# Transposing x1 by DMA in the first three batch entries of a fused linear-attention and FP4-FFN kernel

## The chip, the cores and the metric

The kernel runs on one core of one Trainium2 chip. Its time is the device time of one execution in microseconds (us). Three runs of the kernel before took 1883.41, 1884.52 and 1885.26 us, so the median is 1884.52 us. The core has five engines with a queue each: TensorE (PE in the profile, with its weight loads as PEld), VectorE (DVE), ScalarE (ACT), GpSimd (POOL) and SyncE (SP), which here issues nearly all DMAs. Everything is computed in float32 except the quantized grids.

## The reference

The input `src` has 4 batch entries of 2048 rows and 256 columns. Cut to what matters:

```
xn = (src - mean) / sqrt(var + eps)               # per row
# attention branch
Q, K = elu(xn @ Wq + bq) + 1, elu(xn @ Wk + bk) + 1   # 16 heads of 64
KV = einsum('bshd,bshm->bhdm', K, xn @ Wv + bv)
o  = Q KV / (Q . sum(K) + eps)
x1 = layer_norm(xn + o @ Wo + bo) * g1 + be1
y  = gelu(x1 @ W1 + b1) @ W2 + b2
s  = layer_norm(x1 + y) * g2 + be2
# gate branch: weights and activations quantized to FP4 in blocks of 16
h  = silu(q(xn) @ q(w_gate).T) * (q(xn) @ q(w_up).T)
out = src + s * silu(q(h) @ q(w_down).T)
```

The change bears on `x1`: how its affine part is applied, how it is transposed for `x1 @ W1`, and what is issued around it.

## The kernel before

Rows are worked in 32 blocks of 256 (two tiles of 128 rows, `j` = 0 and 1); a batch entry has 8 blocks. A prologue works the keys of entry 0. Then a loop over `n` = 0 to 31 does the queries, attention and both FFNs of block `n`, and, while there is a next entry, two "subs" of that entry's keys beside it. Each entry has 16 subs: the first eight make the normalized rows `xn_k` and their transpose `xnT_k` (keys of the first 512 features), the last eight load both back from DRAM (second 512 features). So in the blocks before a block with `bi` = 0 to 3 keys are normalized and transposed too; in the other blocks of entries 0 to 2 they are only loaded. Blocks 24 to 31 (the last entry) have no keys beside them.

The order on PE is the order of the program's text (`tc.keep_in_program_order`). In the steady loop VectorE, ScalarE, GpSimd and SP are put in order by a scheduler at build time, with `tc.issue_after` as the author's hints; in the prologue VectorE and ScalarE too keep the program's order. The result is a fixed order per queue: an instruction that waits holds up all that stand behind it on its engine.

Per block PE does, in order and by the names of its PSUM tiles: `pk` (keys), `pz` (row sums for the denominators), `pxk` (keys times rows), `pg` (gate and up), `pd` (down), a second `pk`, `pa` (attention times Wo; by seven products over sums `zs` of VectorE in entries 0 to 2), `pxk`, part of `py` (x1's second FFN product of block `n-1`), `pt_x` (the transposes of x1), `pscale` (the transpose of the FP4 scales), the rest of `py`, `pq` (queries of block `n+1`), `pf` (x1 @ W1). PSUM has eight banks; four of them go round among all `mm` tiles, so `pq` and `pf` also wait until VectorE or ScalarE has read out the tile that had the bank before.

After `pa`, VectorE adds the parts into `x1` (`add_seven`), takes mean and variance (`stats`, with a power on GpSimd for 1/sqrt, tile `rstd`), and normalizes. `x1_T` then transposes the normalized x1 by four PE transposes into `pt_x`, and ScalarE copies it out with scale g1 and bias be1. GpSimd applies the same affine part to the row-major x1 (`ffn_addend`: times g1, plus `shift`, which is be1 + b2). GpSimd also makes `o = g*be2 + x` and `g*g2` for the output (`gate_addend`), and adds bo to xn (`attention_addend`). VectorE uses `o` and `g` in `output_of`.

`keys_apart` and `keys_T` are the way in which 22 of the key tiles are transposed: ScalarE copies the high and low 16-bit halves of the float32 tile apart, a DMA transposes them, and ScalarE puts the halves together again.

Of the kernel before, what the change touches and what calls it, by code (L numbers as in the profile page):

```python
# [8 lines left out]
F32 = mybir.dt.float32  # L9
# [6 lines left out]
P = 128  # L16
LN_EPS = 1e-5
Z_EPS = 1e-6
BLK = 16
# [3 lines left out]
def linear_attention_gated_by_fp4_ffn(  # L23
# [158 lines left out]
    for _ in range(24):  # L182
# [13 lines left out]
    W2_OF = {"11": 0, "21": 1, "22": 2, "t1": 3, "t2": 4, "t3": 5, "t4": 6}  # L196
    row_tiles = {
        name: const.tile([P, 1, D], F32, name=f"{name}_r")
        for name in ("bo", "g1", "shift", "g2", "be2")
    }  # L200
    rows = {name: t.to_broadcast([P, TB, D]) for name, t in row_tiles.items()}

# [3 lines left out]
    def load_row(name, v, dep):  # L206
        load_when(dep, row_tiles[name][:, 0, :], as_rows(v))
# [10 lines left out]
    def w2_sums():  # L218
# [23 lines left out]
            lambda dep: load_row("shift", be1, dep),  # L242
            lambda dep: load_row("g2", g2, dep),
            lambda dep: load_row("be2", be2, dep),
        ],
# [18 lines left out]

    cols = {}

    def add_b2(dep):
        b2_r = work.tile([P, D], F32, tag="s", name="b2_r", bufs=1)
        load_when(dep, b2_r, as_rows(b2))
        shift = row_tiles["shift"][:, 0, :]  # L270
        nc.gpsimd.tensor_tensor(shift, shift, b2_r, ALU.add)

    def small_constants():


        vs = (("b1", b1), ("g1", g1), ("be1", be1))
        n = sum(v.shape[0] // P for _, v in vs)
        brow = work.tile([n, P], F32, tag="z", name="brow", bufs=1)
        r = 0
        for name, v in vs:  # L280
            k = v.shape[0] // P
            nc.sync.dma_start(brow[r : r + k, :], v.rearrange("(c p) -> c p", p=P))
            cols[name] = (r, r + k)
            r += k
        yield
        pb = mm_tile("pb")
        tr(pb[:, :n], brow, ident[:n, :n])
        bcol = const.tile([P, n], F32, name="bcol")
        vector.tensor_copy(bcol, pb[:, :n])
        for name, (lo, hi) in cols.items():  # L290
            cols[name] = bcol[:, lo:hi]
        yield


# [2 lines left out]
    def fp4_scale(x, am, name):  # L297

        nb = x.shape[1]
        rs = small.tile([P, I // BLK], F32, tag="rs", name=f"rs_{name}")[:, :nb]  # L300
        vector.tensor_reduce(am, x, AX.X, ALU.max, apply_absolute_value=True)
        vector.tensor_scalar(am, am, -1.0 / 6.0, -1e-12, ALU.mult, ALU.min)
        vector.reciprocal(rs, am)
        return rs
# [146 lines left out]

    xn_d, xnT_d = {}, {}
    keys = {}

# [42 lines left out]
            nc.sync.dma_start(xn, xn_d[n])  # L499
            nc.sync.dma_start(xnT, xnT_d[n])  # L500

    def keys_apart(b, sub, issue=None):
# [7 lines left out]
        half = keys[b, sub][0].bitcast(U16).rearrange("p j (c f h) -> p h c j f", c=ND, h=2)  # L510
        apart = work.tile([P, 2, ND, TB, P], U16, tag="e", name=f"apart_{n}", bufs=3)
        with tc.issue_after(issue) if issue is not None else nullcontext():
            for h in range(2):
                scalar.copy(apart[:, h], half[:, h])
        apartT = work.tile([P, 2, ND * T], U16, tag="kk", name=f"apartT_{n}", bufs=3)
        nc.sync.dma_start(
            apartT.rearrange("p h (m t) -> p (h m) t", t=P),
            apart.rearrange("p h c j f -> p (h c j f)"),
            transpose=True,
        )  # L520
        keys[b, sub].append(apartT)

    def keys_T(b, sub, issue=None):

        f, bi = divmod(sub, NB)
        if f > 0:
            return
        n = b * NB + bi
        xn, *apartT = keys[b, sub]
        xnT = work.tile([P, ND, T], F32, tag="xnT_k", name=f"xnT_k_0_{n}", bufs=3)  # L530
        if apartT:
            with tc.issue_after(issue):
                scalar.copy(
                    xnT.bitcast(U16).rearrange("p c (t h) -> p h (c t)", h=2), apartT[0]
                )
# [241 lines left out]
    def down(n, j):  # L777
        if j == 0:
            blk[n]["pd"] = acc_tile(f"pd_{n}").rearrange("p (j d) -> p j d", j=TB)
        pd = blk[n]["pd"]  # L780
        for i in range(NI):
            mm(
                pd[:, j, :], qT[:, i, j * P : (j + 1) * P], wd[:, i, :], start=i == 0, stop=i == NI - 1
            )
        if j < TB - 1:
            return
        g = work.tile([P, TB, D], F32, tag="g", name=f"g_{n}")
        scalar.activation(g, pd, AF.Silu)
# [22 lines left out]
    def ffn_addend(n, behind=True):  # L811

        x1 = blk[n]["x1"]
        with tc.issue_after(pool["last"]) if behind else nullcontext():
            nc.gpsimd.tensor_tensor(x1, x1, rows["g1"], ALU.mult)
            pool["last"] = nc.gpsimd.tensor_tensor(x1, x1, rows["shift"], ALU.add).ins


    def q_of(n, chunks=range(NH)):
# [128 lines left out]
            vector.tensor_tensor(x1, xn, pa, ALU.add)  # L948
        blk[n]["x1"] = x1

    def attention_norm(n):
        x1 = blk[n]["x1"]
        mv, rstd = stats(x1, f"1_{n}")
        normalize(x1, x1, mv, rstd)

    def x1_T(n):
        x1 = blk[n]["x1"]
        pt = transposes(x1, f"x1_{n}")
        x1T = work.tile([P, ND, T], F32, tag="x1T", name=f"x1T_{n}", bufs=1)
        for c in range(ND):  # L960
            ins = scalar.activation(
                x1T[:, c, :], pt[:, c, :], AF.Identity,
                bias=cols["be1"][:, c : c + 1], scale=cols["g1"][:, c : c + 1],
            )
        blk[n]["x1T"] = x1T
        blk[n]["act"] = ins.ins

    def ffn_1(n, chunks=range(NF)):
        x1T = blk[n]["x1T"]
# [80 lines left out]
    for n in range(NB):  # L1050
# [47 lines left out]
        ready = weight  # L1098
        if n == 4:
            w_down_sb = load_down()  # L1100
        if n == 5:
            add_b2(dep)
        if n == 6:
            load_xn(0)
            scales_x(0)
# [49 lines left out]
    for n in range(NBLK):  # L1155
        b, bi = divmod(n, NB)
        subs = (2 * bi, 2 * bi + 1) if b + 1 < B else ()
        if n < last:
            gate = gate_up(n + 1)
        if 1 < n < last:  # L1160
            gate_addend(n - 1)
        if subs:
            if n == 0:
# [25 lines left out]
            down(n, 1)  # L1189
        elif n < last:  # L1190
            load_xnT(n + 1)
            block_addends(n)
            with tc.issue_after(quantized_h(n, 0).ins):
                ins = quantized_x(n)
            ins = sums(n, ins.ins)
            down(n, 0)
            with tc.issue_after(ins.ins):
                quantized_h(n, 1)
            step(m_half)
            step(gate, 9)  # L1200
            step(m_half)
            down(n, 1)
        else:
            for j in range(TB):
                quantized_h(n, j)
                down(n, j)
        with tc.issue_after(blk[n + 1]["late"]) if n < last else nullcontext():
            qz_ins = qz(n)
        if in_seven(b):
            attention_sums(n)  # L1210
        if not subs:
            ffn_2(n - 1, 4 if n < last else 8)
        if n == 0:
            attention(n)
        kk_ins = keys_k(b + 1, subs[1]) if subs else qz_ins
        if n > 0:
            with tc.issue_after(kk_ins):
                ffn_sums(n - 1)
            attention(n)
        with tc.issue_after(kk_ins):  # L1220
            attention_norm(n)
        if n + 2 < NBLK:
            load_xn(n + 2)
        if subs:
# [31 lines left out]
        if n > 0:  # L1256
            ffn_2(n - 1, 28)
        if more[0]:
            q_of(n + 1)
        if more[0]:  # L1260
            grid_of_h(n + 1, 0)
            grid_T(n + 1, 0, NI)
# [9 lines left out]
            step(m_half)  # L1272
        for sub in next_subs[:1]:
            keys_T(bn + 1, sub, blk[n + 1]["exp"])
        if n + 1 == last:
            ffn_1(n, range(2))
            sums(last)
            ffn_1(n, range(2, NF))
            gpsimd_behind(blk[n]["hT"][:, NF - 1, :])
            gate_addend(n)  # L1280

            w2_last = wk_sb.rearrange("p c (e d) -> p (c e) d", d=D)
            nc.sync.dma_start(w2_last, by_chunks(W2))
        else:
            ffn_1(n)
# [46 lines left out]
```

## Time and profile before

| | |
|---|---|
| median of three runs | 1884.52 us |
| the profiled execution's own time | 1883.6 us |
| its span | 1881.8 us |
| PE busy | 1860.8 us (99%) |
| VectorE busy | 1381.8 us (73%) |
| ScalarE busy | 706.5 us (38%) |
| GpSimd busy | 382.5 us (20%) |
| granted TensorE clock | 0.999 |

The page's chain of work that ended last lies on PE for 77% of the span. A block of entries 0 to 2 takes about 56.4 us, a block of the last entry 44.4 us (the distance of equal PE rows in the chain). Idle time of an engine that is not on that chain costs nothing by itself. The end of a matmul is modelled in this profile, so a busy PE row can hide a short wait; the starts are measured, and the distance of two starts tells what a matmul took of PE.

### The profile page before, as it was taken

What the parts mean: (1) busy time and instruction counts of PE and PEld (TensorE: products, weight loads), DVE (VectorE), ACT (ScalarE), POOL (GpSimd) and SP (SyncE); (2) the same over time, 40 slices, a digit from 0 to 9 for tenths busy, and PEclk for the clock granted to TensorE, in tenths of its full rate; (3) what the DMA queues carried; (4) which work ended last, traced back from release to release, by engine and by line L of the source; (5) the groups of instructions that cost most, each with busy time, mean ns of one, the idle gap of its engine ahead of it and who ended that gap; (6) DMA issues with size and microseconds to landing.
All of it is one profiled execution on the core that took longest, in us unless ns stands there. A gap on an engine that the chain in (4) does not pass through costs nothing.

```text
span 1881.8 us, 25202 instructions
## 1 busy us (share of the span) xinstructions
PE 1860.8 (99%) x9324; PEld 1382.2 (73%) x9324; DVE 1381.8 (73%) x2524; ACT 706.5 (38%) x1190; POOL 382.5 (20%) x363
## 2 busy tenths in 40 slices
PE   8999999999999999999999999999999999999998
PEld 4456677777777777777777787777777788888887
DVE  5676677766677877777677787776776777888875
ACT  2343544324334335443233543353323333333332
POOL 1411322011122212220112221222101122222212
PEclk9999999999999999999999999999999999999999
DMA  5525655444535456635344654564443444444542
GB/s 182 194 77 127 116 120 102 100 102 94 96 63 99 111 98 122 143 66 110 81 89 79 119 100 104 94 139 90 91 88 71 104 77 83 89 83 84 92 83 50
DMA packets 229433, 188.77 MB, mean 100 GB/s; under 512 B 107687, under 2 KB 191155, under 8 KB 229310
## 3 DMA queue, kind: packets, MB, share of 16 engines
q1 hardware_dynamic: 228476, 185.58, 47.4%
q8 instruction: 74, 1.21, 0.3%
q10 hardware_dynamic: 834, 1.58, 0.3%
q14 instruction: 49, 0.40, 0.1%
HBM read 131.96 MB, written 32.59 MB: 87 GB/s over the span
## 4 chain that ended last, share of the span: by engine, by line
PE 77%; DVE 10%; DMA 9%; SPq 1%; issue 1%; POOL 1%; ACT 1%; POOLq 0%; DVEq 0%; ACTq 0%
PE pg L103 14%; PE pk L103 10%; PE pxk L103 10%; PE pf L103 9%; PE pa L103 8%; PE pq L103 8%; PE pd L103 7%; PE py L103 7%; DMA zb<-z_d 2%; DMA qT<-scale_d 2%; PE pz L103 1%; DMA xn_d<-xn_k 1%; DMA z_d<-z 1%; DVE x L119 1%; POOL rstd L430 1%
## 5 line engine op out<-in xcount | busy, mean ns | idle before, releaser
L430 POOL TENSOR_TENSOR rstd<-rstd,neg_half 128x2 f32<-128x2 f32 (+1 forms) x97 | 77.3, 797 | 1324.8 <-DVE rstd L119 964.9
L103 PE MATMUL pg<-wgu,qT 128*128 128x352 f32 x1024 | 308.5, 459 | 0.2 <-PE pm L103 0.2
L103 PEld LDWEIGHTS pg<-wgu,qT 128*128 128x128 f32 x1024 | 194.3, 190 | 113.8 <-issue 11.5
L103 PE MATMUL pk<-wk_sb,xnT_k 128*128 128x512 f32 x512 | 230.4, 592 | 1.2 <-ACT xnT_k L119 1.2
L103 PE MATMUL pf<-x1T,w_sb 128*128 128x256 f32 x1024 | 227.7, 380 | 2.2 <-DVE zq L119 1.6
L103 PE MATMUL pxk<-kk,xn_k 128*128 128x512 f32 x496 | 227.9, 598 | 1.1 <-DVE kk L119 1.1
L103 PE MATMUL pq<-xnT,wq_sb 128*128 128x256 f32 x1024 | 227.6, 380 | 0.9 <-DVE zq L119 0.8
L103 PEld LDWEIGHTS pf<-x1T,w_sb 128*128 128x128 f32 x1024 | 193.6, 190 | 32.3 <-DVE zq L119 6.0
L103 PEld LDWEIGHTS pq<-xnT,wq_sb 128*128 128x128 f32 x1024 | 191.8, 190 | 27.1 <-DVE zq L119 2.4
L119 DVE SCALAR_TENSOR_TENSOR kk<-ek,pk 128x512 f32<-128x512 f32 x128 | 85.5, 684 | 170.3 <-ACT ek L119 170.3
L103 PE MATMUL pd<-wd,qT 128*128 128x256 f32 x768 | 172.9, 380 | 1.1 <-DVE qT L119 1.1
L119 ACT ACT_TABLE_LOAD x121 | 155.2, 1283 | 49.2 <-PE pk L103 34.3
L103 PEld LDWEIGHTS pk<-wk_sb,xnT_k 128*128 128x128 f32 x512 | 97.0, 190 | 102.6 <-issue 90.3
L119 ACT ACTIVATE x1T<-pt_x,bcol 128x256 f32<-128x256 f32 x64 | 32.6, 560 | 357.8 <-PE pt_x L106 357.8
L103 PEld LDWEIGHTS pd<-wd,qT 128*128 128x128 f32 x768 | 145.3, 190 | 27.9 <-DVE qT L119 4.4
L103 PEld LDWEIGHTS pxk<-kk,xn_k 128*128 128x128 f32 x496 | 89.4, 190 | 99.2 <-issue 87.0
L119 DVE TENSOR_TENSOR h<-h,pg 128x352 f32<-128x352 f32 x128 | 66.0, 516 | 105.4 <-PE pg L103 103.2
L119 ACT ACTIVATE h<-pg 128x352 f32<-128x352 f32 x128 | 58.8, 459 | 211.3 <-PE pg L103 211.2
L119 ACT ACTIVATE hT<-pf,bcol 128x256 f32<-128x256 f32 x256 | 105.7, 471 | 66.0 <-PE pf L103 65.6
L119 DVE TENSOR_TENSOR zq<-zq,zb 128x1024 f32<-128x1024 f32 x64 | 79.2, 1238 | 64.9 <-DMA zb<-z_d 64.5
L103 PE MATMUL py<-w_sb,hs 128*128 128x128 f32 x992 | 122.0, 275 | 0.0
L119 ACT ACTIVATE e<-pq,neg_one 128x512 f32<-128x512 f32 x128 | 86.6, 685 | 84.7 <-PE pq L103 70.6
(159 smaller groups left out, 2789.4 us busy)
## 6 DMA issues: line engine op xcount, KB each, us to landing
zb<-z_d SPq DMA_DIRECT2D x128, 256.0 KB, 6.3
qT<-scale_d SPq DMA_DIRECT2D x248, 128.0 KB, 6.0
x_k<-in_L_attn_src_dram SPq DMA_DIRECT2D x32, 256.0 KB, 4.0
x<-in_L_attn_src_dram SPq DMA_DIRECT2D x32, 256.0 KB, 2.9
xn_d<-xn_k SPq DMA_DIRECT2D x32, 256.0 KB, 2.7
xn<-xn_d SPq DMA_DIRECT2D x32, 256.0 KB, 2.7
xnT_d<-xnT_k SPq DMA_DIRECT2D x32, 256.0 KB, 2.0
xnT<-xnT_d SPq DMA_DIRECT2D x32, 256.0 KB, 4.0
```

The source lines that it names most:

```text
L103: return tc.keep_in_program_order(nc.tensor.matmul(*args, **kw))
L119: ins = op(*args, **kw)
L430: pool["last"] = nc.gpsimd.tensor_tensor(rstd[:, j0:j1], rstd[:, j0:j1], neg_half[:, j0:j1], ALU.pow).ins
```

## The change

1. `x1_T` of blocks 1 to 23 no longer uses PE. ScalarE copies the 16-bit halves of x1 apart (`apart`), one DMA transposes them, and ScalarE puts them together (`x1_together`), in the middle of the query products of the next block. The buffers are parts of the tile `zs`.
2. g1 and be1 are applied by VectorE in `attention_norm`: two `scalar_tensor_tensor` per tile in the place of one `tensor_scalar`. GpSimd only adds b2. Blocks 0 and 24 to 31 still transpose x1 on PE, with one plain copy on ScalarE.
3. Of two keys in one block, the second is copied apart and transposed later, behind the queries; the first takes the third part of the `zs` tile.
4. In the last entry, GpSimd's `gate_addend` waits for the quantized h (`qT`), where it stood behind the previous block's output.
5. In block 0 the FP4 scales of the second tile stand behind the sums `zs`, the key normalization behind x1's, and a one-element Exp on ScalarE follows the Silu of `down`.
6. The last block's attention is done tile by tile (`attention_by_tiles`).

```diff
@@ fp4_scale
-        rs = small.tile([P, I // BLK], F32, tag="rs", name=f"rs_{name}")[:, :nb]
+        rs = small.tile([P, I // BLK], F32, tag="rs", name=f"rs_{name}", bufs=3)[:, :nb]
...
+    def apart(x, xp, xpT):
+        half = x.bitcast(U16).rearrange("p j (c f h) -> p h c j f", c=ND, h=2)
+        for h in range(2):
+            ins = scalar.copy(xp[:, h], half[:, h])
+        nc.sync.dma_start(
+            xpT.rearrange("p h (m t) -> p (h m) t", t=P),
+            xp.rearrange("p h c j f -> p (h c j f)"),
+            transpose=True,
+        )
+        return ins.ins
+
+    def together(xT, xpT, issue):
+        with tc.issue_after(issue):
+            scalar.copy(xT.bitcast(U16).rearrange("p c (t h) -> p h (c t)", h=2), xpT)
...
@@ down
-        scalar.activation(g, pd, AF.Silu)
+        blk[n]["silu"] = scalar.activation(g, pd, AF.Silu).ins
...
@@ ffn_addend
-            nc.gpsimd.tensor_tensor(x1, x1, rows["g1"], ALU.mult)
-            pool["last"] = nc.gpsimd.tensor_tensor(x1, x1, rows["shift"], ALU.add).ins
+            pool["last"] = nc.gpsimd.tensor_tensor(x1, x1, rows["b2"], ALU.add).ins
...
+    def attention_by_tiles(n):
+        x1 = blk[n]["x1"] = work.tile([P, TB, D], F32, tag="x1", name=f"x1_{n}")
+        xn, zq = blk[n].pop("xn"), blk[n].pop("zq")
+        for j in range(TB):
+            pa = (acc_tile, mm_tile)[j](f"pa{j}_{n}")[:, :D]
+            for c in range(NH):
+                mm(
+                    pa, zq[:, c, j * P : (j + 1) * P], m_sb[n // NB, c // FOUR][:, c % FOUR, :],
+                    start=c == 0, stop=c == NH - 1,
+                )
+            vector.tensor_tensor(x1[:, j, :], xn[:, j, :], pa, ALU.add)
+            attention_norm(n, (j,))
+
-    def attention_norm(n):
+    def attention_norm(n, js=range(TB)):
         x1 = blk[n]["x1"]
-        mv, rstd = stats(x1, f"1_{n}")
-        normalize(x1, x1, mv, rstd)
+        mv, rstd = stats(x1, f"1_{n}_{js[0]}", js)
+        for j in js:
+            vector.scalar_tensor_tensor(
+                x1[:, j, :], x1[:, j, :], mv[:, j, 0:1], rows["g1"][:, j, :], ALU.subtract, ALU.mult
+            )
+        for j in js:
+            ins = vector.scalar_tensor_tensor(
+                x1[:, j, :], x1[:, j, :], rstd[:, j : j + 1], rows["be1"][:, j, :], ALU.mult, ALU.add
+            )
+        blk[n]["normal"] = ins.ins
+
+    def x1_by_dma(n):
+        return n > 0 and in_seven(n // NB)
 
     def x1_T(n):
         x1 = blk[n]["x1"]
-        pt = transposes(x1, f"x1_{n}")
-        x1T = work.tile([P, ND, T], F32, tag="x1T", name=f"x1T_{n}", bufs=1)
-        for c in range(ND):
-            ins = scalar.activation(
-                x1T[:, c, :], pt[:, c, :], AF.Identity,
-                bias=cols["be1"][:, c : c + 1], scale=cols["g1"][:, c : c + 1],
-            )
-        blk[n]["x1T"] = x1T
-        blk[n]["act"] = ins.ins
+        x1T = blk[n]["x1T"] = work.tile([P, ND, T], F32, tag="x1T", name=f"x1T_{n}", bufs=1)
+        if x1_by_dma(n):
+            t = work.tile([P, 3, ND * T], F32, tag="zs", name=f"apart_x1_{n}", bufs=1).bitcast(U16)
+            xp, blk[n]["room"] = (
+                t[:, i].rearrange("p (h c j f) -> p h c j f", h=2, c=ND, j=TB) for i in (0, 2)
+            )
+            blk[n]["apart"] = t[:, 1].rearrange("p (h t) -> p h t", h=2)
+            blk[n]["act"] = apart(x1, xp, blk[n]["apart"])
+        else:
+            blk[n]["act"] = scalar.copy(x1T, transposes(x1, f"x1_{n}")).ins
+
+    def x1_together(n, issue):
+        if x1_by_dma(n):
+            together(blk[n]["x1T"], blk[n].pop("apart"), issue)
...
@@ loop over n
-        if 1 < n < last:
+        if 1 < n < last and subs:
             gate_addend(n - 1)
...
         elif n < last:
             load_xnT(n + 1)
+            ins = quantized_h(n, 0)
+            gpsimd_behind(qT[:, 0, :])
+            gate_addend(n - 1)
             block_addends(n)
-            with tc.issue_after(quantized_h(n, 0).ins):
+            with tc.issue_after(ins.ins):
                 ins = quantized_x(n)
...
         if n == 0:
             attention(n)
+            one = small.tile([1, 1], F32, tag="one", name="one_exp")
+            with tc.issue_after(blk[n]["silu"]):
+                scalar.activation(one, neg_one[:1], AF.Exp)
...
-            attention(n)
-        with tc.issue_after(kk_ins):
-            attention_norm(n)
+            if n < last:
+                attention(n)
+            else:
+                attention_by_tiles(n)
+        if n < last:
+            with tc.issue_after(kk_ins):
+                attention_norm(n)
...
-            with tc.issue_after(qz_ins) if not subs else nullcontext():
+            behind = zs_ins if n == 0 else None if subs else qz_ins
+            with tc.issue_after(behind) if behind is not None else nullcontext():
                 scales_h(n + 1, 1)
...
+        x1_T(n)
         for sub in next_subs if n == 0 else ():
-            keys_in(bn + 1, sub)
-        x1_T(n)
+            with tc.issue_after(blk[n]["normal"]):
+                keys_in(bn + 1, sub)
...
-        for sub in next_subs:
-            keys_apart(bn + 1, sub, blk[n]["act"])
+        room = blk[n].pop("room", None)
+        for sub in next_subs[:1]:
+            keys_apart(bn + 1, sub, blk[n]["act"], room)
...
-            q_of(n + 1)
+            q_of(n + 1, range(NH // 2))
+            x1_together(n, blk[n + 1]["exp"])
+            q_of(n + 1, range(NH // 2, NH))
...
+        for sub in next_subs[1:]:
+            keys_apart(bn + 1, sub, blk[n + 1]["exp"])
```

Left out are the row tiles (`be1` and `b2` loaded as two rows in the place of their sum `shift`), the smaller table of column constants, and `keys_apart` and `keys_T`, which now call `apart` and `together`.

More of the change, by code (lines that the diff above doesn't have):

```diff
@@ L198, in linear_attention_gated_by_fp4_ffn @@
         name: const.tile([P, 1, D], F32, name=f"{name}_r")
-        for name in ("bo", "g1", "shift", "g2", "be2")
+        for name in ("bo", "g1", "be1", "b2", "g2", "be2")
     }
@@ L241, in linear_attention_gated_by_fp4_ffn @@
             lambda dep: load_row("g1", g1, dep),
-            lambda dep: load_row("shift", be1, dep),
+            lambda dep: load_row("be1", be1, dep),
+            lambda dep: load_row("b2", b2, dep),
             lambda dep: load_row("g2", g2, dep),
@@ L265, in linear_attention_gated_by_fp4_ffn @@
     cols = {}
[L267 to L271, printed above, removed]
-    def small_constants():
[L276 to L284, printed above, removed]
+    def small_constants():
+        brow = work.tile([NF, P], F32, tag="z", name="brow", bufs=1)
+        nc.sync.dma_start(brow, b1.rearrange("(c p) -> c p", p=P))
         yield
         pb = mm_tile("pb")
[L287 to L291, printed above, removed]
+        tr(pb[:, :NF], brow, ident[:NF, :NF])
+        cols["b1"] = const.tile([P, NF], F32, name="bcol")
+        vector.tensor_copy(cols["b1"], pb[:, :NF])
         yield
@@ L500, in keys_in, with keys_apart @@
             nc.sync.dma_start(xnT, xnT_d[n])
-    def keys_apart(b, sub, issue=None):
+    def keys_apart(b, sub, issue=None, xp=None):
         f, bi = divmod(sub, NB)
@@ L509, in keys_apart @@
         n = b * NB + bi
-        half = keys[b, sub][0].bitcast(U16).rearrange("p j (c f h) -> p h c j f", c=ND, h=2)
-        apart = work.tile([P, 2, ND, TB, P], U16, tag="e", name=f"apart_{n}", bufs=3)
+        if xp is None:
+            xp = work.tile([P, 2, ND, TB, P], U16, tag="e", name=f"apart_{n}", bufs=3)
+        apartT = work.tile([P, 2, ND * T], U16, tag="kk", name=f"apartT_{n}", bufs=3)
         with tc.issue_after(issue) if issue is not None else nullcontext():
[L513 to L519, printed above, removed]
-        )
+            apart(keys[b, sub][0], xp, apartT)
         keys[b, sub].append(apartT)
@@ L531, in keys_T @@
         if apartT:
[L532 to L535, printed above, removed]
+            together(xnT, apartT[0], issue)
         else:
@@ L1100, in linear_attention_gated_by_fp4_ffn @@
             w_down_sb = load_down()
-        if n == 5:
-            add_b2(dep)
         if n == 6:
@@ L1209, in linear_attention_gated_by_fp4_ffn @@
         if in_seven(b):
-            attention_sums(n)
+            zs_ins = attention_sums(n)
         if not subs:
@@ L1248, in linear_attention_gated_by_fp4_ffn @@
             gate_addend(n)
-        for sub in next_subs:
-            keys_apart(bn + 1, sub, blk[n]["act"])
+        room = blk[n].pop("room", None)
+        for sub in next_subs[:1]:
+            keys_apart(bn + 1, sub, blk[n]["act"], room)
+        room = None
         if n > 0 and not subs:
```

## The prediction

> **What bounds the kernel now.** I read the page's busy times first, then PE's waits, then the timeline of one block.
>
> ```profile
> span 1881.8 us, 25202 instructions
> ...
> PE 1860.8 (99%) x9324; PEld 1382.2 (73%) x9324; DVE 1381.8 (73%) x2524; ACT 706.5 (38%) x1190; POOL 382.5 (20%) x363
> ```
>
> PE is busy 99%, VectorE 73%. The waits of PE alone (columns: us in total, times, longest):
>
> ```profile
> PE pa L103 <- DVE zs L119: 2.4, 3, 1.6
> ...
> PE pf L103 <- DVE zq L119: 1.6, 3, 0.8
> ...
> PE pt_x L106 <- DVE x L119: 1.1, 3, 0.5
> ```
>
> All of PE's visible waits come to some 14 us, so what is taken out of PE's queue shortens the run unless a wait takes its place. The timeline of block 3 (start, length):
>
> ```profile
> 360.70 0.73 DVE L119 TENSOR_SCALAR x<-x,mv,rstd 128x256 f32<-128x256 f32 x2 [0.81 <-POOL rstd L430]
> 361.32 1.95 PE L103 MATMUL py<-w_sb,hs 128*128 128x128 f32 x16
> ...
> 363.11 0.60 PE L106 MATMUL pt_x<-ident,x 128*128 128x128 f32 x4
> 363.55 0.27 PE L106 MATMUL pscale<-ident,scale 128*128 128x128 f32 x1
> ...
> 365.44 7.07 PE L103 MATMUL pq<-xnT,wq_sb 128*128 128x256 f32 x32
> ...
> 372.35 1.89 PE L103 MATMUL pf<-x1T,w_sb 128*128 128x256 f32 x8
> ```
>
> From 361.3 to 379 PE has no gap. The four transposes take 363.55 - 363.11 = 0.44 us, 0.109 us each by their starts. x1 was ready at 361.43 and is wanted, transposed, at 372.35: there is room for a slower way.
>
> [...] But the starts carry no slack: 32 `pq` matmuls follow each other every 6.91/32 = 0.216 us. [...]
>
> **1. Transposes out of PE, blocks 1 to 23.** 23 x 0.436 = 10.0 us. PE also waited for x1 in five of these blocks (starts at 479, 536, 881, 939 and 1342 us): 0.26 + 0.37 + 0.60 + 0.58 + 0.84 = 2.65 us. Nothing on PE needs x1 there any more, so I count 12.7 us.
>
> What has to hide instead, with the block above and PE 0.44 earlier after the transposes:
> - VectorE: four operations like `s<-s,mv,g` for two like `x<-x,mv,rstd`, some 1.1 us a block on an engine that is busy 73%; uncovered, 25 us over these blocks.
>
> ```profile
> L119 DVE SCALAR_TENSOR_TENSOR s<-s,mv,g 128x256 f32<-128x256 f32 x62 | 30.2, 492 | 0.0
> ...
> L119 DVE TENSOR_SCALAR x<-x,mv,rstd 128x256 f32<-128x256 f32 x64 | 23.5, 410 | 20.4 <-POOL rstd L430 20.4
> ```
>
> In the changed order one g1 operation stands ahead of the power's input (+0.42), the other beside the power (+0.15, see 3), two be1 operations behind it (+0.17), and `y` moves behind x1 (-0.61). x1 is ready near 361.6.
> - ScalarE copies the halves apart: 1.14 us a pair in this trace. To 362.8.
> - The DMA. The nearest row is that of the keys' halves, of the same shape:
>
> ```profile
> L516 SPq DMA_TRANSPOSE apartT<-apart x22: 1231/1241/1552, 197.3 to 1230.3; - x22
> L119 ACT COPY xnT_k<-apartT x22: 1324/1332/1363, 203.6 to 1245.0; 128x1024 uint16<-128x1024 uint16 x22
> ...
> DMA to landing us min/median/max: 3.4/3.9/4.5
> ```
>
> It lands at 366.2 to 367.3. The copy that joins the halves stands behind the second Exp of the queries (done 369.4), takes 1.33, and x1T is there at 370.7. `pf` would start at 371.9. Slack 1.2 us, and 2 to 3 us in the DMA before the join is late.
> - ScalarE's extra 1.14 + 1.33 - 1.02 = 1.45 us a block lies in its waits (38% busy); uncovered it would cost 33 us. The join delays the third Exp by about 0.3 us; `pf`'s third bank waits for it, with 0.5 us to spare.
> - SP issues one transpose more, 1.24 us, ahead of the scale DMAs. Those start some 0.5 us later and land near 377 (last issue 370.3, 6.0 to land); the product on VectorE that wants them starts at 384.2.
> - The second key's halves leave after the output's store. In block 2 that puts the landing near 326, where the joining copy is due on ScalarE; what stands behind it, the Silu of `pg`, ran at 332.3. Nothing.
> - VectorE's order changes: in 13 blocks (3 to 6, 11 to 14, 19 to 23) all of the output's additions precede the first `zq`, and the output's last operations, 1.42 us each beside GpSimd, stand between the last `zq`s. `pf` needs the banks that `zq` frees. Placing these rows, the third and fourth `zq` end 0.5 and 0.2 us before the bank is wanted. This is the thinnest cover: 0 to 0.8 us a block. I take 0.1, the rows' own scatter: +1.3 us.
> - GpSimd loses 32 operations of 1.27 us; nobody waits for them, 0. Row loads, buffers and column constants: prologue, hidden by its PE work; 0, and at most 1 us.
>
> **2. Block 0.**
>
> ```profile
> 180.18 2.05 PE L103 MATMUL pa<-m,zs 128*128 128x128 f32 x16 [1.55 <-DVE zs L119]
> ...
> 188.58 3.70 PE L103 MATMUL pxk<-kk,xn_k 128*128 128x512 f32 x8 [1.12 <-DVE kk L119]
> ...
> 200.58 1.99 PE L103 MATMUL pf<-x1T,w_sb 128*128 128x256 f32 x8 [0.77 <-DVE zq L119]
> ```
>
> The second tile's maximum, scale and reciprocal leave the way of `zs`: 1.25 of the 1.55. The table load (1.28) ahead of `ek` goes: 1.12. Then x1's chain is late for its transposes, which were just in time: -1.0. Two copies and a wait for a store leave the way of the queries' Exp: some 0.9 of 0.77 + 0.43. Together 2.3 us; bounds 0 (the chain takes it all back) and 4.
>
> **3. The last entry, blocks 24 to 30.** Here x1 is still transposed on PE, and there was no slack:
>
> ```profile
> 1601.49 0.73 DVE L119 TENSOR_SCALAR x<-x,mv,rstd 128x256 f32<-128x256 f32 x2 [0.81 <-POOL rstd L430]
> ...
> 1602.15 0.68 PE L106 MATMUL pt_x<-ident,x 128*128 128x128 f32 x4
> ...
> 1615.51 2.89 DVE L119 SCALAR_TENSOR_TENSOR o<-s,rstd,o 128x256 f32<-128x256 f32 x2
> ...
> 1620.40 2.86 PE L103 MATMUL pd<-wd,qT 128*128 128x256 f32 x12 [0.18 <-DVE qT L119]
> ```
>
> x1 ends at 1602.22 and the transposes are issued at 1602.15 (they take 0.08 more than 0.436). Whatever makes x1 later is a wait of PE. It becomes later by one g1 operation ahead of the power's input, 0.42 at the rate of successive rows; by the power being slower beside the other g1 operation; and by the be1 pair, 0.90 for 0.73: +0.17. For the power the trace has the same picture in the output's part: at 1614.61, beside an `s<-s,mv,g` that ends at 1614.92, it takes 0.87, alone (1600.75) 0.70: +0.17. [...]
>
> Against it: GpSimd's three operations move behind `qT`, so the pair `o`, 2.89 us beside them, falls toward 0.9 and the wait of `pd` on `qT` (0.25 by its starts) goes; one operation less beside `y` frees the 0.25 that `pf` waits for `zq`. Net 0.15 a block, 7 x 0.15 = +1.0 us; bounds -3.5 (only the gains) and +4.6 (only the loss).
>
> **4. The last block.** PE waits 0.97 us for x1. By tiles the second tile's chain is that of `s_last` at the end, 2.6 us from addition to result (1876.09 to 1878.70), against 3.45 before (1856.41 to 1859.85): 0.85 us less. The end behind the last matmul stays.
>
> **Sum.** -12.7 + 1.3 - 2.3 + 1.0 - 0.85 = -13.5 us. The profiled execution took 1883.6 us (1881.8 span and 1.8 around it): 1870.1. The median of the runs is 0.9 above it: 1871.0. Bounds of these terms: block 0 from 0, the banks at 13 x 0.8, the last entry at +4.6 would give 1886; all the good ends some 1863.
>
> **Rivals.**
> *The cover is too thin.* The third and fourth `zq` come after the slow `o`s, `pf` waits 0.4 us in 13 blocks (+3.9), the last entry loses its 4.6 without the gain (+3.6), block 0 gains nothing (+2.3): 1881. For it: slacks of 0.2 to 0.5 us read off rows of another order. Against it: the `o`s collide with GpSimd one at a time once a `zq` lies between them.
>
> *x1 comes late by DMA (slower).* Place: `pf` on x1T, 23 times. The join must start by 370.5, so the DMA may take 7.7 us from its issue at 362.8. The rows of `gridT`, also transposed, land after 8.0 us in the median, because they stand behind eight `qT` transfers. Above a wait of 13.5/23 = 0.59 us a block, that is 8.3 us to landing, the change loses. At 9.0 us it costs 1.3 x 23 = 30: 1901. Against it: in the changed order x1's DMA stands ahead of the scale transfers, and behind nothing issued in the last 3 us but, in some blocks, a key tile of 2.7 us.
>
> *No change.* PE is early, but a chain through VectorE sets the block (`zs` behind the queries' denominators, the waits of 2.4 us above grow): 12.7 is eaten by 0.5 a block, 1884. Little speaks for it: most blocks wait nowhere on VectorE.
>
> That the transposes stay on PE is excluded by the order of the changed program: `pt_x` is gone from 23 blocks.
>
> **How the numbers follow.** A measurement of this kernel can tell about 0.2% from no change, 3.8 us. My own case (1866 to 1876) 0.60; thin cover (1876 to 1881) 0.20; no change 0.05; slower 0.15. Faster 0.80, same 0.05, slower 0.15. The range takes in the thin cover and the same: 1865 to 1885. The likeliest is 1871.
>
> **What would show it.** Right: `pt_x` x36 in the page, PE about 12 us less busy, blocks of entries 0 to 2 at 56.0 us from `pf` to `pf`, x1's DMA landing in about 4 us, `pf` without a wait for ACT x1T; `pt_x` waiting on DVE in seven blocks of the last entry, 0.65 each, while the wait of `pd` there is gone; no 1.5 us wait at block 0's `zs`. Wrong: `pf` waits for x1T or `zq` in most blocks, or a block of the last entry takes more than 45 us.

## The result, and the profile after

The changed kernel takes 1892.3 us (median of eight runs, 1885.6 to 1894.0), the kernel before beside it 1884.4: ratio 1.0039, 95% interval 1.0029 to 1.0049. It is slower by 0.4%; predicted were 1871 us. The kernel before had medians of 1884.4, 1883.2, 1881.9 and 1882.2 us beside the runs that follow, so two kernels of different experiments can be compared to some 2 us; the ratios are to the kernel before that ran beside them. The profiled execution took 1892.25 us. Its page, and the row of the query products (busy and mean | idle before, what ended most of it):

```profile
span 1890.5 us, 25109 instructions
...
PE 1856.3 (98%) x9232; PEld 1372.5 (73%) x9232; DVE 1375.7 (73%) x2590; ACT 732.9 (39%) x1205; POOL 351.0 (19%) x338
...
L103 PE MATMUL pq<-xnT,wq_sb 128*128 128x256 f32 x1024 | 233.0, 383 | 16.5 <-DVE zq L119 11.1
```

PE has 92 transposes less to do, 10 us of work, and the run is longer: PE now waits. Its waits, as for the kernel before (us in total, times, longest):

```profile
PE pq L103 <- DVE zq L119: 11.1, 10, 2.1
PE pq L103 <- DVE s L119: 5.4, 8, 1.3
...
PE pf L103 <- DVE zq L119: 0.5, 1, 0.5
PE pt_x L106 <- DVE x L119: 0.3, 1, 0.3
```

The wait is at a place that the prediction did not look at: the fourth query product (`pq` of chunk 6), in 18 of the blocks 1 to 23. By the starts, each distance less the 0.216 us of a matmul, these waits are 19.5 us; the kernel before had 1.5 there. There is no wait of `pf` for x1T. When PE's time in blocks 1 to 23 is summed from start to start, by the tile that starts, the change is -12.8 us at `pt_x`, -1.6 at `pa`, +20.5 at `pq` and +4.3 at `pf`: together the 10.5 us by which these blocks are longer (table below). Most of what in the 20.5 and 4.3 is not waiting is slow work behind the waits (last section). The fourth query product is the first that needs a PSUM bank again that was in use just before. In blocks 3 to 6, 11 to 14 and 19 to 23 (no keys are normalized there) it takes the bank of py's second half, free when VectorE has done the last of five additions `s`. In blocks 1, 2, 7 to 10 and 15 to 18 (with key normalization) it takes the bank of the first query product, free after the first `zq`; what releases PE in the trace shows it. The timeline of block 5, of the first kind:

```profile
477.85 0.69 DVE L119 SCALAR_TENSOR_TENSOR y<-xn,rs_x 128x512 f32<-128x512 f32 x1
...
478.02 1.14 ACT L119 COPY apart_x<-x 128x512 uint16<-128x512 uint16 x2 [13.31 <-PE py L103]
...
479.16 0.79 ACT L119 ACTIVATE m_h<-h 128x704 bf16<-128x704 f32 x1
...
479.66 5.35 PE L103 MATMUL pq<-xnT,wq_sb 128*128 128x256 f32 x24
...
479.97 0.89 DVE L119 SCALAR_TENSOR_TENSOR h<-m_h,h 128x704 f32<-128x704 bf16 x1 [1.44 <-ACT m_h L119]
...
482.19 0.75 DVE L119 SCALAR_TENSOR_TENSOR grid<-m_x,y 128x256 bf16<-128x256 bf16 x2
482.86 0.68 DVE L119 TENSOR_TENSOR s<-x,py 128x512 f32<-128x512 f32 x1
...
483.57 2.12 DVE L119 TENSOR_TENSOR s<-s,py 128x384 f32<-128x384 f32 x4
...
485.61 0.68 DVE L119 SCALAR_TENSOR_TENSOR zq<-e,pq 128x512 f32<-128x512 f32 x1
485.84 1.97 PE L103 MATMUL pq<-xnT,wq_sb 128*128 128x256 f32 x8 [0.83 <-DVE s L119]
```

VectorE stands idle for 1.44 us, because `m_h` on ScalarE is queued behind the copies of x1's halves. The five `s` come after that, though the first two could have run in the gap (py's first half was done; e6 below moves them there). They end at 485.7; PE wanted the bank at 479.66 + 24 x 0.216 = 484.84. In block 7, of the second kind, the way is longer. First the changed kernel, then the kernel before:

```profile
594.31 5.35 PE L103 MATMUL pq<-xnT,wq_sb 128*128 128x256 f32 x24
...
595.81 0.73 DVE L119 TENSOR_SCALAR xn_k<-x_k,mv,rstd 128x256 f32<-128x256 f32 x2 [0.58 <-POOL rstd L416]
...
597.26 0.68 DVE L119 SCALAR_TENSOR_TENSOR y<-xn,rs_x 128x512 f32<-128x512 f32 x1
...
598.04 0.63 ACT L119 ACTIVATE m_x<-y 128x512 bf16<-128x512 f32 x1 [4.40 <-DVE y L119]
...
599.83 1.26 ACT L119 ACTIVATE e<-pq,neg_one 128x512 f32<-128x512 f32 x2
...
600.45 0.55 DVE L119 TENSOR_TENSOR s<-s,py 128x384 f32<-128x384 f32 x1
...
600.91 0.68 DVE L119 SCALAR_TENSOR_TENSOR zq<-e,pq 128x512 f32<-128x512 f32 x1
...
601.65 2.83 PE L103 MATMUL pq<-xnT,wq_sb 128*128 128x256 f32 x8 [1.99 <-DVE zq L119]
```

```profile
591.88 0.69 DVE L119 SCALAR_TENSOR_TENSOR y<-xn,rs_x 128x512 f32<-128x512 f32 x1
...
593.15 0.73 DVE L119 TENSOR_SCALAR xn_k<-x_k,mv,rstd 128x256 f32<-128x256 f32 x2 [0.58 <-POOL rstd L430]
...
594.65 7.30 PE L103 MATMUL pq<-xnT,wq_sb 128*128 128x256 f32 x32
...
599.23 1.48 DVE L119 SCALAR_TENSOR_TENSOR zq<-e,pq 128x512 f32<-128x512 f32 x2
```

In the changed kernel `y` stands behind both key normalizations; before, it stood ahead of the second. ScalarE waits 4.40 us for it at `m_x`, and the Exp of the first query product (its input was complete at 594.31 + 8 x 0.216 = 596.0) is queued behind `m_x` and the key's copies and runs at 599.8. But that Exp is not what comes last. It ended at 600.5, and VectorE reached the first `zq` 0.4 us later, since the additions `s`, the second `y` and the grids of x stand between. In all ten such blocks the Exp had ended (by 0.03 to 1.1 us) when the first `zq` started, and from `y` to that `zq` VectorE never paused for more than 0.3 us. Before, between the second key normalization and the first `zq`, VectorE stood idle for 0.3 to 2.0 us in each of these blocks: that was the slack, and most of it is used up.

The stages, from the first row-sum product `pz` of one block to that of another, in us:

| kernel | prologue | block 0 | blocks 1 to 23 | 24 to 30 | 31 and end |
|---|---|---|---|---|---|
| before | 153.2 | 58.6 | 1315.8 | 307.5 | 46.6 |
| after | 153.9 | 57.4 | 1326.3 | 308.3 | 44.6 |
| difference | +0.7 | -1.3 | +10.5 | +0.8 | -2.0 |

The differences add up to the 8.7 us by which the spans differ. The prologue's 0.7 is no more than its scatter from one profile to another (153.0 to 154.6 in the ten that follow).

### The profile page after: what moved, and what is told of

Read it like the earlier page. It is cut to its first block, busy times and chain, and to the rows that moved or that the text cites. A ratio compares the mean times of both kernels' runs of the same rounds, so it can differ in the third digit from the quotient of the medians.

```text
span 1890.5 us, 25109 instructions
## 1 busy us (share of the span) xinstructions
PE 1856.3 (98%) x9232; PEld 1372.5 (73%) x9232; DVE 1375.7 (73%) x2590; ACT 732.9 (39%) x1205; POOL 351.0 (19%) x338
## 4 chain that ended last, share of the span: by engine, by line
PE 57%; DVE 19%; DMA 11%; issue 7%; POOL 3%; SPq 1%; ACT 1%; POOLq 0%; DVEq 0%; ACTq 0%
PE pf L103 10%; PE pg L103 10%; PE pk L103 8%; PE pxk L103 8%; PE pd L103 6%; PE pq L103 6%; PE pa L103 5%; DMA zb<-z_d 4%; DMA xn<-xn_d 3%; PE py L103 3%; POOL rstd L416 3%; DVE x L119 3%; DVE hs L119 2%; DMA z_d<-z 2%; DVE scale L119 2%
## 5 line engine op out<-in xcount | busy, mean ns | idle before, releaser
L416 POOL TENSOR_TENSOR rstd<-rstd,neg_half 128x2 f32<-128x2 f32 (+1 forms) x98 | 84.8, 865 | 1327.7 <-DVE rstd L119 1262.3
L103 PE MATMUL pq<-xnT,wq_sb 128*128 128x256 f32 x1024 | 233.0, 383 | 16.5 <-DVE zq L119 11.1
L119 ACT ACTIVATE hT<-pf,bcol 128x256 f32<-128x256 f32 x256 | 105.1, 474 | 58.4 <-PE pf L103 57.4
L119 ACT ACTIVATE ek<-pk,neg_one 128x512 f32<-128x512 f32 x128 | 85.5, 686 | 83.4 <-PE pk L103 79.0
```

Of the source, the lines that this page charges most:

```text
L103: return tc.keep_in_program_order(nc.tensor.matmul(*args, **kw))
L119: ins = op(*args, **kw)
L416: pool["last"] = nc.gpsimd.tensor_tensor(rstd[:, j0:j1], rstd[:, j0:j1], neg_half[:, j0:j1], ALU.pow).ins
```

## The experiments

The theory after this reading: the new way of x1 is early enough, and the loss is VectorE's and ScalarE's order, which hands back PSUM banks late. Rivals: the DMA itself, VectorE's extra work for g1 and be1, parts 4 to 6. The edits are shown shortened.

**e1 and e2: another bank.** The edit, in the changed kernel and, as a control, in the kernel before:

```diff
-            kinds = (mm_tile, acc_tile) if n >= NBLK - NB - 1 else (acc_tile, mm_tile)
+            kinds = (mm_tile, acc_tile)
```

> The changed kernel, with the two PSUM tiles of py exchanged between the pools in all blocks (first bank from the four `mm` banks, second from `acc`). The order of the instructions is the same on all five engines; only the bank that the fourth query product (pq of chunk 6) takes differs: that of py's first half, free after the second of the five output additions, where it was free after the fifth (13 blocks) or after the first zq (10 blocks). Theory 'bank': the 19.5 us of waits at the fourth query product are the whole loss, and nothing behind them is late; then they fall to about 1 us, the clock drop behind the two longest waits (3.4 us) goes too, and the run takes about 1870 us. Theory 'VectorE late': VectorE's fixed order is late as a whole, and the wait moves to pf, whose third bank wants the third zq, which stands behind an `o`; with VectorE's instructions left where the trace has them I count 9.0 us there and 12.5 us in all, so the run takes about 1880 us. Rival 'DMA': x1T comes late; then pf waits for x1T as soon as PE is earlier, and the time stays within 3 us of 1892.

> Control: the same exchange of py's PSUM tiles in the kernel before. Again only banks differ, no order. Theory 'bank': the kernel before waits 1.1 us in all at the fourth query product, so it gains 1 us at most: 1883 to 1884.5. Rival: the exchange is good or bad by itself (py's first half now waits for another bank): more than 3 us either way.

e1 took 1880.1 us (ratio to before 0.9981, 0.9974 to 0.9988), 12 us less than the changed kernel (11 by the ratios), with the order on PE, VectorE, ScalarE and GpSimd the same instruction for instruction. So the loss goes through this bank. But it isn't the 1870 of the simple theory; it is the 1880 of the second one. e1's waits, and its block 5:

```profile
PE pf L103 <- DVE zq L119: 7.7, 11, 1.1
...
PE pf L103 <- ACT x1T L119: 1.2, 3, 0.6
...
PE pq L103 <- DVE s L119: 0.2, 1, 0.2
```

```profile
487.21 1.48 DVE L119 SCALAR_TENSOR_TENSOR o<-s,rstd,o 128x256 f32<-128x256 f32 x1 [0.58 <-POOL rstd L416]
...
488.61 0.68 DVE L119 SCALAR_TENSOR_TENSOR zq<-e,pq 128x512 f32<-128x512 f32 x1
489.21 0.89 DVE L119 SCALAR_TENSOR_TENSOR o<-s,rstd,o 128x256 f32<-128x256 f32 x1
489.34 3.72 PE L103 MATMUL pf<-x1T,w_sb 128*128 128x256 f32 x16 [0.81 <-DVE zq L119]
```

PE is now early at the queries and waits at the third bank of `pf`: the third `zq` stands behind an `o` that waits 0.58 us for the power and takes 1.48 beside GpSimd. The first wait had hidden the second. e2 took 1881.3 us (0.9990, 0.9982 to 0.9998): the exchange is worth some 1.9 us in the kernel before, slightly more than expected, and not 12. There, too, no order changed.

**e3 and e4: the change in halves.** e3 undoes the DMA, e4 takes parts 4 to 6 into the kernel before.

```diff
     def x1_by_dma(n):
-        return n > 0 and in_seven(n // NB)
+        return False
```

> The changed kernel, with x1 transposed on PE in all blocks (one plain copy out of PSUM); g1 and be1 stay on VectorE and parts 4 to 6 stay. Theory 'bank' (both forms): with pt_x back in the round of banks, zq stands between the output's additions again and the fourth query product waits for next to nothing; the transposes cost 10.0 us again and x1 is late at pt_x in about ten blocks by some 0.4 us: 1886 us. If VectorE's extra work by itself were the loss, the time stays at 1892 or above, as the transposes come on top. If the DMA by itself were the loss, it falls below the kernel before: 1882 or less.

> The kernel before with parts 4 to 6 of the change alone: the gate's addends behind qT in the last entry, block 0 reordered, the last attention by tiles; g1 and be1 stay with ScalarE and GpSimd, x1 is transposed on PE. Expected: in the last entry the waits of pd and pf (0.25 each) go in six or seven blocks and x1 is no later, -3 us; block 0 gives -1; the last block -0.7: 1879.7 us. Rival: the addends behind qT come late for the output's o, and what is won at pd is lost at zq: 1883.

e3 took 1885.6 us (1.0018, 1.0012 to 1.0025), as expected, but not for the reason given. `pt_x` waits hardly anywhere in blocks 1 to 23; instead the fourth query product waits in the ten blocks with key normalization, 8.9 us by the starts. In the other blocks, where two `s` run ahead of `h`, it waits nowhere. So part of the loss comes without the DMA, with g1 and be1 on VectorE. Here `y` stands ahead of the second key normalization, as before; but that normalization starts 1.3 us later against the queries than before (mean of the ten blocks), about what the extra operations take, and the Exp had ended 1.0 to 2.0 us when VectorE reached the first `zq`. In blocks 1 to 23 e3 takes 1321.5 us, 5.7 more than before.

e4 took 1882.5 us (0.9996, 0.9988 to 1.0004), 3 us more than expected. The last entry gave 0.5 us where 3 were expected (a wait of 1.4 us at `pscale` took most), and block 0 lost: 61.3 us for 58.6, with a wait of 2.85 us at `pf`. Parts 4 to 6 neither make nor hide the loss. Blocks 1 to 23 took 2.2 us less than before, with the same order on PE, VectorE and ScalarE: so much two profiled executions can differ there.

**e5: besides the banks, the output's o behind zq.** The edit to e1:

```diff
-            vector.scalar_tensor_tensor(zq[:, cc : cc + 2, :], e, 1.0, pq, ALU.min, ALU.max)
+            ins = vector.scalar_tensor_tensor(zq[:, cc : cc + 2, :], e, 1.0, pq, ALU.min, ALU.max)
+            blk[n]["zq_at", cc] = ins.ins
...
+        with tc.issue_after(blk[n + 2]["zq_at", 6]):
             for j in js:
                 vector.scalar_tensor_tensor(o[:, j, :], s[:, j, :], rstd[:, j : j + 1], o[:, j, :], ALU.mult, ALU.add)
```

> The kernel with py's PSUM tiles exchanged, and besides VectorE's two o of the output behind the fourth zq (in 11 of the 13 blocks where one o stood between the third and the fourth zq, and one ahead of the third). Theory 'VectorE's order': the 7.7 us that pf waits for zq in 11 blocks, with 0.2 to 0.3 us of slow matmuls behind each, are all that is left of the loss: 1880.1 - 7.7 - 2.5 = 1870. Rival 'VectorE full': the o late pushes the keys' kk or the next scales, and PE waits there; the time stays above 1877.

e5 took 1866.7 us, ratio to before 0.9924 (0.9911 to 0.9936). It beats both kernels. Its waits:

```profile
PE pf L103 <- ACT x1T L119: 1.0, 2, 0.6
...
PE pf L103 <- DVE zq L119: 0.5, 1, 0.5
```

Nothing is left at `pq`. Blocks 1 to 23 take 1302.6 us, 13.2 less than before; VectorE is as busy as in the changed kernel (1377.8 for 1375.7 us), and `y` still stands behind the keys. "VectorE full" is out: VectorE as late as that costs PE nothing where PE does not need its bank so early.

**e6: two additions into VectorE's idle gap.** The changed kernel with its own banks; `output`, now the five additions alone, is traced ahead of the grids, and the rounding of h and of x is issued behind the second of them (`two`):

```diff
+        if n > 0:
+            output(n - 1)
         if more[0]:
             grid_of_h(n + 1, 0)
...
-            grid_of_h(n + 1, 1, blk[n]["act"])
+            grid_of_h(n + 1, 1, blk[n]["act"], blk[n - 1]["two"])
...
         if n > 0:
-            output(n - 1)
+            output_rest(n - 1)
```

> The changed kernel with its own banks; the first two additions of the output stand ahead of the rounding of h on VectorE (issue_after), where VectorE stood idle for 1.44 us waiting for m_h. Theory 'VectorE's order': in the blocks without key normalization the fifth addition comes 1.2 us earlier, the eight waits of the fourth query product for s (6.7 us) fall under 0.5 us, with some 3 us of slow matmuls behind them; the ten waits for zq in the blocks with key normalization stay: 1882. Rival 'VectorE full': the idle 1.44 us is not what delays the additions, the waits for s stay above 4 us and the time within 3 us of 1892.

e6 took 1873.4 us (0.9958, 0.9945 to 0.9970), where 1882 was expected. The waits for `s` are gone, as expected. Its waits for `zq` fell too, to 5.1 us in five blocks, which was not expected: the edit changes VectorE's order in the ten blocks with key normalization as well.

**e7: without g1 and be1.**

```diff
-            vector.scalar_tensor_tensor(x1[:, j, :], x1[:, j, :], mv[:, j, 0:1], rows["g1"][:, j, :], ALU.subtract, ALU.mult)
...
-            ins = vector.scalar_tensor_tensor(x1[:, j, :], x1[:, j, :], rstd[:, j : j + 1], rows["be1"][:, j, :], ALU.mult, ALU.add)
+            ins = vector.tensor_scalar(x1[:, j, :], x1[:, j, :], mv[:, j, 0:1], rstd[:, j : j + 1], ALU.subtract, ALU.mult)
```

> The changed kernel without g1 and be1 (left out altogether: the affine part of the first layer norm is not applied; one tensor_scalar per tile normalizes, as in the kernel before). x1 still goes by DMA, banks and the rest as changed. It tells the two halves of the change apart. Theory 'both': in the blocks with key normalization y stands ahead of the keys again, e_0 no longer waits behind m_x, and the 12.6 us of waits for zq fall to 2 or less; in the others the five additions stay ahead of zq, and 4 us of waits for s stay, with those of pf behind them; the last entry's 0.3 + 0.35 us at pt_x go in seven blocks (-4): 1873. Rival 'affine harmless, DMA alone': above 1887. Rival 'affine alone': no wait left at the fourth query product or pf, 1868 or less.

e7 took 1884.0 us (1.0011, 1.0003 to 1.0019), where "both" said 1873; its profiled execution, at 1879.2, was the fastest of its 13 runs, so the rows below are its best case. Its waits:

```profile
PE pf L103 <- DVE zq L119: 6.8, 11, 0.6
PE pq L103 <- DVE s L119: 2.7, 6, 1.2
PE pq L103 <- DVE zq L119: 2.5, 4, 1.1
```

The waits for `zq` at the queries fell from 11.1 to 2.5 us and those for `s` to 2.7, as "both" said. The last entry fell by 4.1 us against the changed kernel, as expected. The 6.8 us at `pf` were not in that sum: in the ten blocks with key normalization both `o` stand ahead of the fourth `zq`. With e3: the affine without the DMA costs 5.7 us in blocks 1 to 23 against before, the DMA without the affine 3.8 (1319.6 us, in its best case), both 10.5. Neither half is harmless. Part 3 was in all three, and no run undoes it alone; it is in e5 too, which loses nothing.

**e8: the last entry's affine back on ScalarE and GpSimd.** On top of e5:

```diff
+        if not in_seven(n // NB):      # x1: plain normalization on VectorE
+            ins = vector.tensor_scalar(x1[:, j, :], x1[:, j, :], mv[:, j, 0:1], rstd[:, j : j + 1], ALU.subtract, ALU.mult)
...
+                    ins = scalar.activation(x1T[:, c, :], pt[:, c, :], AF.Identity, bias=cols["be1"][:, c : c + 1], scale=cols["g1"][:, c : c + 1])
...
+            if not in_seven(n // NB):
+                nc.gpsimd.tensor_tensor(x1, x1, rows["g1"], ALU.mult)
```

> The kernel of e5 (banks exchanged, o behind zq), and the last entry with x1's affine part as in the kernel before: ScalarE applies g1 and be1 while it copies x1T, GpSimd multiplies by g1 and adds be1 + b2. In the last entry pt_x waits 0.31 + 0.35 us for x1 in seven blocks; with x1 earlier the block falls from 44.35 to the 44.12 us that it had with parts 4 to 6 alone: 1.6 us less than e5, 1868. If x1's lateness there costs nothing, the same as e5.

Blocks 24 to 30 take 306.3 us, 2.1 less than in e5 (expected 1.6); the seven profiles that have the changed kernel's last entry, g1 and be1 included, lie between 307.9 and 309.0. The median is 1866.6 us, ratio 0.9916 (0.9903 to 0.9930); by the runs alone it can't be told from e5.

**e9 and e10: what the DMA is worth, and whether o alone would do.** e9 is e5 with e3's edit; e10 is the changed kernel with e5's edit and its own banks.

> The kernel of e5 (banks exchanged, o behind zq) with x1 transposed on PE in all blocks again. It asks what the DMA itself is worth once nothing on VectorE is in PE's way. Theory: the four transposes of 0.436 us in 23 blocks, 10.0 us, and little else: 1866.7 + 10.0 = 1877. Rival 'the DMA's room was needed': with pt_x back, x1 comes late at it by some 0.4 us in ten blocks: 1881. Rival 'the gain of e5 is that of the exchange and the order alone': within 3 us of 1867.

> The changed kernel with its own banks, only the two o of the output behind the fourth zq. It asks whether the order of o alone would do. Theory: the waits at the fourth query product (19.5 us) stand ahead of o and stay; the 0.24 us that pf waits in eight blocks go: 1890. Rival 'o is the cause of both': under 1880.

e9 took 1875.8 us (0.9966, 0.9954 to 0.9979): 9.1 us more than e5 by the medians, 7.9 by the ratios, 8.6 in blocks 1 to 23 of the profiles. The transposes on PE are worth nearly what their count says, 10.0 us, once nothing is in PE's way. So of the 15.2 us (1881.9 - 1866.7) that e5 gains, 8 to 9 are the DMA's; the other 6 or 7 are the order, the banks and the rest of the change. e10 took 1885.7 us (1.0017, 1.0008 to 1.0025), where 1890 was expected: 12.7 us of idle time at the fourth query product stay, of the 16.5 in the changed kernel's page. Why they are 4 us less is open; where VectorE stands when a block begins changes with the block before.

## Why the prediction was wrong

**Transposes out of PE: right.** Predicted 10.0 us and 2.65 of waits for x1, 12.7 together; from the changed kernel's queue 12.8 went at `pt_x`. What that is worth when nothing takes its place, by e5 and e9, is 8 to 9 us. So the sum was right to count 0.44 us a block.

**x1 by DMA in time: right.** The tile `apart_x` of the changed kernel (duration min/median/max; then the time from issue to landing):

```profile
L446 SPq DMA_TRANSPOSE apart_x<-apart_x x23: 1232/1253/2466, 248.6 to 1520.8; - x23
...
DMA to landing us min/median/max: 2.7/2.8/5.2
```

In block 3 the copies apart ended at 362.9 (predicted 362.8), x1T at 370.2 (370.7) and `pf` started at 371.4 (371.9): a slack of 1.3 us, predicted 1.2. The DMA was quicker than the keys' row (2.8 us for 3.9).

**The failed step: "VectorE's order changes".** The prediction named it the thinnest cover and took 0.1 us in 13 blocks, +1.3 us; the 1.1 us a block of g1 and be1 on VectorE it took as hidden. Four things were wrong.
- It looked at `pf`'s banks alone; the fourth query product needs a bank too, and earlier.
- It took the 13 blocks with all `s` ahead of `zq` for the only ones. In the ten others the extra work and `y` behind the keys make VectorE late for the first `zq`: 11.1 us of the waits in the page.
- The move of `y` was counted as a gain of 0.61 us for x1, and what stands behind `y` on VectorE was not followed.
- It placed the third and fourth `zq` 0.5 and 0.2 us ahead of need; in e1, where the bank in front is out of the way, `pf` waits for the third in eight of the 13 blocks (6.9 of the 7.7 us).

In its place: 19.5 us of waits in blocks 1 to 23, and what follows each wait (last section). Predicted for these blocks -11.4, measured +10.5; with the order mended and the banks exchanged (e5) -13.2.

**The rival "the cover is too thin"** had the mechanism, but at `pf`, in 13 blocks, at 0.4 us. "x1 comes late by DMA" was wrong. "No change" named a chain through VectorE and dismissed it because before most blocks waited nowhere on VectorE: the absence of waits in the kernel before said nothing of the slack behind them. Both gave times below the measured one, 1881 and 1884 us. The signs that were named for being wrong did not come: `pf` waits in one block, and the last entry's blocks take 44.4 us. A sign of being right did not come either: a block of entries 0 to 2 takes 57.7 us in the mean, where 56.0 was named; before it was 57.2 in the mean, since not all take the 56.4 of the shortest.

**Block 0:** predicted -2.3, measured -1.3. The wait at `zs` shrank by 1.28 (predicted 1.25), but `kk` still costs 0.72 for 1.12. By the starts `pt_x` is 0.7 us later (predicted 1.0), `pf` 1.0 earlier (predicted 0.9), and a wait of 1.0 us at `pg`, for which the profile names no releaser, is new; e5 does not have it.

```profile
180.30 2.05 PE L103 MATMUL pa<-m,zs 128*128 128x128 f32 x16 [0.28 <-DVE zs L119]
...
188.30 3.70 PE L103 MATMUL pxk<-kk,xn_k 128*128 128x512 f32 x8 [0.72 <-DVE kk L119]
```

**The last entry:** predicted +1.0, measured +0.8. As said, the waits of `pd` for qT and of `pf` for `zq` are gone, but for one, and `pt_x` waits for x1: it starts 0.31 us late, and the next row of PE follows at 1613.14, 0.78 us later for 0.436, since the second tile is waited for again. That is 0.65 us, as predicted. The predicted figure was the author's estimate: 0.42 + 0.17 + 0.17 from rows of the kernel before, less some 0.1, a term that no row shows by itself; measured is the 0.65 as a whole. The seven blocks together: +4.0 us at `pt_x`, -1.1 at `pd`, -2.1 at `pf`.

```profile
1610.75 0.48 DVE L119 SCALAR_TENSOR_TENSOR x<-x,mv,g_r 128x256 f32<-128x256 f32 x1
1610.92 0.87 POOL L416 TENSOR_TENSOR rstd<-rstd,neg_half 128x2 f32<-128x2 f32 x1 [21.66 <-DVE rstd L119]
...
1611.82 0.88 DVE L119 SCALAR_TENSOR_TENSOR x<-x,rstd,be_r 128x256 f32<-128x256 f32 x2 [0.59 <-POOL rstd L416]
1612.36 0.94 PE L106 MATMUL pt_x<-ident,x 128*128 128x128 f32 x4
```

For the power beside the other g1 operation the prediction took +0.17, from one row of the kernel before (0.87 us beside VectorE, 0.70 alone). Here it is beside three operations of VectorE (the first pair of the kernel before, the second of the changed one, the third above):

```profile
591.88 0.69 DVE L119 SCALAR_TENSOR_TENSOR y<-xn,rs_x 128x512 f32<-128x512 f32 x1
591.95 1.17 POOL L430 TENSOR_TENSOR rstd<-rstd,neg_half 128x2 f32<-128x2 f32 x1 [1.20 <-DVE rstd L119]
...
594.34 0.89 DVE L119 SCALAR_TENSOR_TENSOR h<-m_h,h 128x704 f32<-128x704 bf16 x1
594.51 1.26 POOL L416 TENSOR_TENSOR rstd<-rstd,neg_half 128x2 f32<-128x2 f32 x1 [0.93 <-DVE rstd L119]
```

VectorE's operation has 0.62, 0.72 and 0.31 us left when the power starts, and the power ends 0.55, 0.54 and 0.56 us behind it. Against the 0.70 alone it took 0.47, 0.56 and 0.17 us more: in these three rows what the other had left, less some 0.15 us. The size that went into the sum, 0.17, was right.

**The last block:** predicted -0.85, measured -2.0 with the end behind it. PE's wait of 0.97 us for x1 is gone but for 0.1: -0.83 at `pt_x`, as predicted. The rest was not foreseen: -0.45 at `pa`, -0.37 at `pz` and -0.37 behind the last matmul, which the prediction said would stay.

## What to carry to other kernels

A wait that isn't there shows no slack: before work is taken off the bounding engine, list for each PSUM bank that it takes next who must read the bank's last content, and where that reader stands in its queue. That queue's idle time ahead of the reader is the slack, and new work on that engine has to fit into it. Where a queue's order is fixed at build time, moving one operation (`y`) moves all that stands behind it, so follow those readers too. And when one wait is removed, ask which comes next: here `pf` behind `pq`; both together were worth 22 to 26 us (changed kernel to e5, by the ratios and by the medians).

## What was not expected of the hardware

A wait of PE cost more than itself here. After the wait of 2.15 us in block 7, the granted clock fell to 0.50. The windows of that stretch (length; busy time of PE, PEld, DVE, ACT, POOL; granted clock; DMA share; GB/s):

```profile
601.50:602.50 1.00, 0.85 (x4) 0.78 (x5) 1.00 (x4) 1.00 (x2) 0.00 (x0) 1.00 1.46 184
602.50:603.50 1.00, 1.00 (x5) 0.79 (x4) 0.97 (x4) 0.36 (x1) 0.00 (x0) 0.58 0.63 76
603.50:604.50 1.00, 1.00 (x4) 0.81 (x3) 1.00 (x5) 0.00 (x0) 0.00 (x0) 0.50 1.11 137
604.50:606.10 1.60, 1.60 (x5) 1.23 (x5) 1.02 (x4) 1.59 (x2) 1.10 (x2) 0.51 1.13 129
606.10:607.50 1.40, 1.40 (x8) 1.24 (x7) 1.40 (x2) 1.37 (x4) 1.32 (x2) 1.00 1.19 117
```

The matmuls that began between 602.6 and 606.0 took up to 0.427 us for 0.216, 1.7 us more in all. The same followed the 2.06 us of block 16 (up to 0.427 us a matmul again, 1.7 us more) and the two longer waits of e3 and e4 (2.7 and 2.9 us; both profiled executions have a mean granted clock of 0.998, that of the kernel before 0.999). It did not follow the wait of 2.25 us in block 10, nor the other 15 of the changed kernel's 18 waits, of 0.34 to 1.62 us. Behind every one of the 18 waits the first matmul took 0.29 to 0.32 us, 0.1 more than the 0.216 of the next. Of the changed kernel's eight runs the two with a mean granted clock of 0.997 were the slowest (1893.9 and 1894.0 us), the one with 1.000 the fastest (1885.6): that the half clock comes in some executions and not in others, and is a part of the scatter, is the author's estimate from these.
